# A four-layer network on one core: layer 1's preparation for batch 0 placed inside layer 0, and layer 2's first chunk prepared inside layer 1

## The chip, the cores and the metric

The kernel runs on one core of one Trainium2 chip. A core has five engines that run side by side, each with its own in-order stream of instructions: PE (TensorE, matrix products and transposes), DVE (VectorE), ACT (ScalarE), POOL (GpSimd) and SP (SyncE, which here only starts transfers). The metric is device time in microseconds of one execution; lower is better. Before the change it is 15601.95 us, the median of three runs (15600.6 to 15609.41).

## What is computed

The input is a map of 2 batches x 64 x 64 positions x 128 channels, kept as 8192 tokens of 128 numbers in float32. Four layers follow each other, and each adds its result to the map. The parts that this change touches, cut to what matters:

```python
# layer 0: group norm, projection, 3x3 depthwise convolution, then selective scans in four orders
h = dA * h + (dt * ut)[..., None] * bt          # one step of a scan, 16 states a channel, 4096 steps
y = (y - mu) * lax.rsqrt(var + eps) * ln_w + ln_b   # "layer 0's last norm"
x = x + (y * silu(z)) @ W_out.T
# layer 1: deformable 3x3 convolution on the group-normed map
offsets = conv3x3(gn(x), offset_w) + offset_b   # 9 sampling points (dy, dx) a position
val = sum over the 4 neighbours of each point: x[yi, xi] * weight
x = x + einsum('bhwkc,kcf->bhwf', val, kernel) + bias
# layer 2: layer norm of each token, then a scan over 256 channels x 256 states ...
xs = ln(t) @ W_in;  delta, B, C = xs @ W_delta, xs @ W_B, xs @ W_C
state = dA_i * state + dB_i * x_i
# ... a spectral convolution; layer 3: linear attention and a mixture of experts
```

Layer 0 treats the batches one after the other. Layer 1's sampling points of a batch need only that batch's result of layer 0.

## The kernel before the change

All text below uses the line numbers of the kernel before (L598 is line 598). The map lives in SBUF as `X`, 64 tiles of 128 tokens, 32 for each batch.

**Layer 0** (`layer0`) runs per batch `b`: a preparing stage (pools `l0p`, `l0w`: transposes, group norm, projections, the depthwise convolution, which fills `U`), the scans (pools `l0h`, `l0s`, `l0k`; an order written out by hand with `tc.manual_schedule()`), and the last norm (pools `l0f`, `l0fs`; functions `centred` and `projected`, 8 blocks of 512 tokens), which writes `X`, at L457 last. `U` is in a pool that stays for the whole layer; `Y`, the sum of the scans, has a pool of its own for each batch and lies above `U`.

**Layer 1** (`layer1`). For each batch the sampling points are made first (pool `l1p`). Transposes of `X` to channels (`to_channels`, L95, L72, L74), the bias is added to `X` (L521), group norm, transposes back to `xk` (L531), eight transfers of `xk` to a table in HBM (L539, 1 MB each in rows of 512 bytes, on SP's queue), the offset convolution (L548), and some thirty small DVE operations (L570 to L587) that end in `idx`, the table rows to fetch, and `wt`, the weights. Then comes the gather loop over the 64 tiles of tokens: nine indirect transfers from the table by POOL (L598, 128 rows of 2 KB each) into one of four buffers `G`; a DVE product with `wt` (L605); 36 PE transposes that add the four neighbours up (L612), copied out by ACT (L613); nine PE products with the kernel (L616), added to `X` by DVE (L617). At tile 36 the program also makes layer 2's mixing weights (`mixing_weights`, L693 to L711, DVE).

**Between layers 1 and 2**, `norm_tokens` takes mean and variance of all 64 tiles (L629, L630), then one set of small operations makes `rs` and `sh`; `move` (L1410) stores `X` to `x1` in HBM. Layer 2 opens its pools over the place of `X`, and `prologue` for its first chunk of 512 tokens loads `x1`, normalises, transposes, multiplies by four weights in turn (L797, L813, L822; the weights come one after the other through one buffer `w`, L806) and gives `g`, `cv`, `ea` and, through HBM, `drow`. After that `load_row` (L1127, SP) and `make_inputs` (L1139, POOL, 8.9 us) feed the first scan step (L1195, DVE).

**What sets the order.** Outside the blocks with an order written out by hand, the framework puts instructions on each engine by readiness in its own model of time, with the program's order as the priority; so independent work may be mixed. Memory is a stack of pools; a pool opened with `side="right"` takes its place from the other end. A pool that is opened on the place of a closed one waits for the use of the old one; how strictly is a question of the prediction.

Of the kernel before, what the change touches and what calls it, by code (L numbers as in the profile page):

```python
# [16 lines left out]
F32 = mybir.dt.float32  # L17
# [141 lines left out]
def layer0(k):  # L159
# [3 lines left out]
    with ExitStack() as es:  # L163
        enter = es.enter_context
        cst = enter(tc.tile_pool(name="l0c", bufs=1))
        big = enter(tc.tile_pool(name="l0b", bufs=1))
# [28 lines left out]
        U = big.tile([P, 2, L], F32, name="U")  # L195
        zs = dr.tile([2, P, B * L], F32, name="zs")

        for b in range(B):
            Xb = X[:, b * NTB : (b + 1) * NTB, :]
            with ExitStack() as e2:  # L200
# [43 lines left out]
            yb = es.enter_context(ExitStack())  # L244
            Y = yb.enter_context(tc.tile_pool(name=f"l0y{b}", bufs=1)).tile([P, 2, L], F32, name="Y")
# [175 lines left out]

            with ExitStack() as e2:
# [42 lines left out]
                projected(7, *behind)  # L465
            yb.close()
# [23 lines left out]
def layer1(k, table, mix):  # L490
# [3 lines left out]
    with ExitStack() as es:  # L494
        enter = es.enter_context
        cst = enter(tc.tile_pool(name="l1c", bufs=1))
        gp = enter(tc.tile_pool(name="l1g", bufs=4))
# [4 lines left out]
        over = enter(ExitStack())  # L502
        pre = over.enter_context(tc.tile_pool(name="l1p", bufs=1))
        w_k = cst.tile([P, 9, C], F32, name="w_k")
        nc.sync.dma_start(out=w_k, in_=ins["kern1"].rearrange("t c f -> c t f"))
        gmat = cst.tile([P, P], F32, name="gmat1")
        nc.sync.dma_start(out=gmat, in_=ins["gmat"])
        w_o = cst.tile([P, 9, 32], F32, name="w_o")
        nc.vector.memset(w_o, 0.0)
        nc.sync.dma_start(out=w_o[:, :, :18], in_=ins["offw1"].rearrange("t c f -> c t f"))  # L510
        wts, idxs = [], []
        bases = []
        for b in range(B):
            bases.append(pre.tile([P, 2, NTB, 9], F32, name="base", bufs=2))
            nc.sync.dma_start(out=bases[b], in_=ins["base"][:, :, b * NTB : (b + 1) * NTB, :])
        for b in range(B):
            Xb = X[:, b * NTB : (b + 1) * NTB, :]
            xt = pre.tile([P, L], F32, name="xt1")
            to_channels(k, ps, xt, lambda i: Xb[:, i, :], NTB)

            nc.vector.tensor_tensor(Xb, Xb, k.r("bias1").unsqueeze(1).to_broadcast([P, NTB, C]), ALU.add)  # L521
            xp = pre.tile([P, 66, 66], F32, name="xp1")
            zero_frame(nc, xp)
            groupnorm(k, pre, ps, gmat, xt, "gn1")
            nc.scalar.copy(xp[:, 1:65, 1:65], xt.rearrange("p (h w) -> p h w", w=WW))

            xk = pre.tile([P, NTB, C], F32, name="xk")
            for g in range(0, NTB, 4):
                pt = ps.tile([P, N], F32, name="pt1", tag="ps")
                for j in range(4):  # L530
                    nc.tensor.transpose(pt[:, j * P : (j + 1) * P], xt[:, (g + j) * P : (g + j + 1) * P], k.ident)  # L531
                k.copy(xk[:, g : g + 4, :].rearrange("p a c -> p (a c)"), pt)
            cells = table[b].rearrange("(y x) c -> y x c", x=TS)
            for j in range(4):
                dy, dx = divmod(j, 2)
                for yy in range(2):
                    y0 = 2 - dy + yy
                    dst = cells[y0 : y0 + 63 : 2, 2 - dx : 66 - dx, j * C : (j + 1) * C]
                    nc.sync.dma_start(out=dst.rearrange("t x c -> x t c"), in_=xk[64 * yy : 64 * yy + 64, :, :])  # L539

            off = pre.tile([P, NTB, 18], F32, name="off")
            for g in range(2):
                po = ps.tile([P, N], F32, name="po1", tag="ps")
                for t in range(9):
                    ky, kx = divmod(t, 3)
                    for j in range(4):
                        q = 4 * g + j
                        nc.tensor.matmul(po[32 * j : 32 * j + 32, :], w_o[:, t, :], xp[:, 8 * q + ky : 8 * q + ky + 8, kx : kx + WW], start=t == 0, stop=t == 8)  # L548
                ot = pre.tile([P, N], F32, name="ot1", bufs=2)
                k.copy(ot, po)  # L550
                pt = ps.tile([P, N], F32, name="pt2", tag="ps")
                for i in range(4):
                    nc.tensor.transpose(pt[:, i * P : (i + 1) * P], ot[:, i * P : (i + 1) * P], k.ident)
                nc.vector.tensor_tensor(
                    off[:, 16 * g : 16 * g + 16, :].rearrange("p (j i) o -> p j i o", i=4),
                    pt.rearrange("p (i j o) -> p j i o", j=4, o=32)[:, :, :, :18],
                    k.r("offset_b").unsqueeze(1).unsqueeze(1).to_broadcast([P, 4, 4, 18]),
                    ALU.add,
                )

            base = bases[b]
            cell = pre.tile([P, 2, NTB, 9], F32, name="cell")
            frac = pre.tile([P, 2, NTB, 9], F32, name="frac")
            rest = pre.tile([P, 2, NTB, 9], F32, name="rest")
            pt = pre.tile([P, NTB, 9], F32, name="point")
            ti = pre.tile([P, NTB, 9], I32, name="ti")
            tf = pre.tile([P, NTB, 9], F32, name="tf")
            offs = off.rearrange("p t (o a) -> p a t o", a=2)
            for a in range(2):
                nc.vector.tensor_tensor(pt, base[:, a], offs[:, a], ALU.add)  # L570

                nc.vector.tensor_copy(ti, pt)
                nc.vector.tensor_copy(tf, ti)
                nc.vector.tensor_tensor(rest[:, a], tf, pt, ALU.is_gt)
                nc.vector.tensor_tensor(tf, tf, rest[:, a], ALU.subtract)
                nc.vector.tensor_tensor(frac[:, a], pt, tf, ALU.subtract)
                nc.vector.tensor_scalar(rest[:, a], frac[:, a], -1.0, 1.0, ALU.mult, ALU.add)
                nc.vector.tensor_scalar(cell[:, a], tf, -2.0, 64.0, ALU.max, ALU.min)
            nc.vector.tensor_scalar(cell[:, 0], cell[:, 0], float(TS), float(2 * TS + 2), ALU.mult, ALU.add)
            nc.vector.tensor_tensor(tf, cell[:, 0], cell[:, 1], ALU.add)  # L580
            idx = cst.tile([P, NTB * 9], I32, name=f"idx{b}")
            nc.vector.tensor_copy(idx, tf.rearrange("p t o -> p (t o)"))
            wt = cst.tile([P, NTB * 9, 4], F32, name=f"wt{b}")
            for j in range(4):
                wy = (frac if j // 2 else rest)[:, 0]
                wx = (frac if j % 2 else rest)[:, 1]
                nc.vector.tensor_tensor(wt[:, :, j], wy.rearrange("p t o -> p (t o)"), wx.rearrange("p t o -> p (t o)"), ALU.mult)  # L587
# [977 lines left out]
```

## Time and profile before

The profiled execution took 15611.47 us; its span, from the first to the last instruction, is 15609.7 us, so 1.8 us lie around it. The median of the three timed runs is 15601.95 us. All times on the page count from the span's start.

| stretch, us | what runs | length, us |
|---|---|---|
| 0 to 2136 | layer 0, batch 0 (its last norm from 2073) | 2136 |
| 2136 to 4259 | layer 0, batch 1 (its last norm from 4196) | 2123 |
| 4259 to 4330 | layer 1 before its first gather | 71 |
| 4330 to 5316 | the 576 gathers, with all that goes beside them | 986 |
| 5316 to 5339 | the last tiles are used up | 23 |
| 5339 to 5400 | `norm_tokens`, `prologue` of layer 2's first chunk, first `make_inputs` | 61 |
| 5400 to 15300 | layer 2 | 9900 |
| 15300 to 15610 | layer 3 | 310 |

Over the span DVE is busy 88%, POOL 86%, PE 76% and ACT 63%. In a list of groups, a row gives the line, the engine, the operation, output<-inputs, the shapes, the count, then the busy time with the mean of one in ns, and the idle time ahead of them with what ended it. In a timeline a row gives start, length, engine, line, operation, names, count, and in brackets the idle time of the engine and what released it.

### The profile page before, as it was taken

The numbers are of one execution on the slowest core, as the hardware profiler recorded it, in microseconds if no ns is written. First come the engines' busy times: TensorE is split into PE (matmuls) and PEld (weight loads), VectorE is DVE, ScalarE is ACT, GpSimd is POOL, SyncE is SP. The second block draws the span as 40 slices with busy tenths as digits, with TensorE's granted clock in tenths as the row PEclk, the third lists the DMA queues.
The fourth block names the chain that finished last, engine by engine and source line by source line (L and its number), as shares of the span: only waits on it lengthen the run. The fifth ranks groups of instructions, "written<-read, shape, count | busy, mean of one in ns | idle before, by whom it ended". The sixth has DMA issues, their size and how long they took to land.

```text
span 15609.7 us, 191436 instructions
## 1 busy us (share of the span) xinstructions
PE 11894.2 (76%) x69838; PEld 7117.6 (46%) x69838; DVE 13768.3 (88%) x12194; ACT 9829.7 (63%) x15891; POOL 13474.0 (86%) x5144
## 2 busy tenths in 40 slices
PE   6666676666677645486976978979788899898897
PEld 2222232222367512154653645646445555555565
DVE  7999979999853499999999999999999999999964
ACT  5666646666410177777777777777777777777752
POOL 6888848888578699999999999999999999999960
PEclk9999999999988767697987989989999999999998
DMA  2111111211175445465655556656666666666643
GB/s 82 71 71 70 67 60 71 73 68 71 63 226 160 137 151 163 154 195 177 204 188 169 195 179 194 202 182 200 194 193 195 192 197 202 192 196 199 188 160 130
DMA packets 1211438, 2373.47 MB, mean 152 GB/s; under 512 B 346744, under 2 KB 923896, under 8 KB 1044352
## 3 DMA queue, kind: packets, MB, share of 16 engines
q1 hardware_dynamic: 1163072, 2206.74, 43.2%
q0 software_dynamic: 46560, 153.18, 3.3%
q8 instruction: 552, 9.04, 0.2%
q14 instruction: 390, 3.19, 0.1%
q10 hardware_dynamic: 864, 1.32, 0.0%
HBM read 2018.49 MB, written 342.41 MB: 151 GB/s over the span
## 4 chain that ended last, share of the span: by engine, by line
POOL 35%; PE 14%; DVE 11%; DMA 3%; ACT 2%; issue 2%; SPq 0%; POOLq 0%; ACTq 0%; DVEq 0%
POOL S L1139 34%; DVE S L1195 10%; PE pef L1023 7%; PE Z L1157 2%; PE acc L996 2%; DMA row<-drow 2%; PE pw L822 1%; POOL S L1145 1%; ACT dA L1193 1%; ACT ze L1163 1%; DMA w<-in_w_b_dram 0%; PE acc L1058 0%; DMA e<-mdr 0%; ACT e L1003 0%; DMA w<-in_w_c_dram 0%
## 5 line engine op out<-in xcount | busy, mean ns | idle before, releaser
L1195 DVE TENSOR_TENSOR_SCAN S<-dA,S 128x512 f32<-128x512 f32 x8192 | 9226.4, 1200 | 397.2 <-ACT dA L1193 208.2
L1139 POOL TENSOR_TENSOR S<-row,g 128x4096 f32<-128x4096 f32 x1024 | 9102.2, 8895 | 280.6 <-DMA row<-drow 232.4
L1193 ACT ACTIVATE dA<-row,a_t 128x512 f32<-128x512 f32 x8192 | 5616.2, 692 | 2158.3 <-DVE S L1195 2123.3
L1157 PE MATMUL Z<-S,cv 128*32 128x256 f32 x32768 | 2504.9, 436 | 1486.0 <-ACT ze L1163 1227.3
L1023 PE MATMUL pef<-hk,ur 128*128 128x256 f32 x14336 | 3507.0, 388 | 137.8 <-ACT e L1003 122.0
L1023 PEld LDWEIGHTS pef<-hk,ur 128*128 128x128 f32 x14336 | 2642.0, 191 | 1076.6 <-issue 562.1
L376 POOL TENSOR_TENSOR S<-du,br 128x1024 f32<-128x1024 f32 x1024 | 2409.7, 2356 | 282.7 <-DVE M L401 164.9
L387 DVE TENSOR_TENSOR_SCAN S<-dA,S 128x1024 f32<-128x1024 f32 x1024 | 2338.0, 2283 | 161.2 <-ACT dA L385 101.9
L1157 PEld LDWEIGHTS Z<-S,cv 128*32 128x32 f32 x32768 | 1002.0, 121 | 2695.7 <-issue 1286.1
L419 PE MATMUL yp<-M,ident 128*128 128x512 f32 x4096 | 1974.5, 604 | 2.9 <-DVE M L401 2.9
L419 PEld LDWEIGHTS yp<-M,ident 128*128 128x128 f32 x4096 | 789.9, 193 | 2147.7 <-issue 2112.7
L385 ACT ACTIVATE dA<-dt,an 128x511 f32<-128x511 f32 x2048 | 1406.5, 687 | 194.2 <-DVE S L387 148.1
L401 DVE TENSOR_TENSOR M<-S,pcn 128x1024 f32<-128x1024 f32 x1024 | 1250.4, 1221 | 151.9 <-PE pcn L343 51.9
L343 PE MATMUL pcn<-cs,sel 80*128 80x512 bf16 x1024 | 394.7, 385 | 1183.6 <-DVE M L401 1174.7
L1163 ACT COPY ze<-Z 128x512 f32<-128x512 f32 x1024 | 1123.0, 1097 | 236.9 <-PE Z L1157 204.6
L996 PE MATMUL acc<-e,mw 128*128 128x512 f32 x1920 | 1047.6, 634 | 31.2 <-ACT e L1003 30.5
L598 POOL DMA_INDIRECT G<-table,idx x576 | 810.8, 1408 | 202.6 <-issue 170.3
L1023 PEld LDWEIGHTS pef<-hd,ur 128*128 128x128 f32 x4096 | 758.2, 194 | 491.5 <-issue 236.0
L1023 PE MATMUL pef<-hd,ur 128*128 128x256 f32 (+1 forms) x4096 | 877.8, 341 | 101.6 <-ACT e L1003 95.3
L389 ACT COPY stt<-S 128x2 f32<-128x2 f32 x896 | 169.3, 189 | 1067.9 <-DVE S L387 1064.8
L605 DVE TENSOR_TENSOR G<-G,wt 128x4608 f32<-128x4608 f32 x64 | 317.6, 4963 | 579.6 <-DMA G<-table,idx 486.4
L613 ACT COPY vt<-pv 128x512 f32<-128x512 f32 (+1 forms) x192 | 88.4, 480 | 864.9 <-remote 598.0
(331 smaller groups left out, 8503.8 us busy)
## 6 DMA issues: line engine op xcount, KB each, us to landing
row<-drow SPq DMA_DIRECT2D x1024, 1024.0 KB
br<-bc SPq DMA_DIRECT2D x256, 1024.0 KB
zd<-ze SPq DMA_DIRECT2D x1024, 256.0 KB
hk<-in_phi_dram SPq DMA_DIRECT2D x128, 576.5 KB
hk<-in_phi_dram SPq DMA_DIRECT2D x96, 704.5 KB
hd<-in_phi_dram SPq DMA_DIRECT2D x512, 128.5 KB
mw<-wdr SPq DMA_DIRECT2D x480, 128.0 KB
hk<-in_phi_dram SPq DMA_DIRECT2D x160, 320.5 KB
```

The source lines that it names most:

```text
L376: nc.gpsimd.tensor_tensor(S, du, br[:, n % 4, :].unsqueeze(1).to_broadcast([P, 2, T]), ALU.mult)
L385: nc.scalar.activation(dA[:, h, rest], dt[:, h, rest], AF.Exp, scale=an[:, kk * 2 + h, n : n + 1])
L387: nc.vector.tensor_tensor_scan(flat, dflat, flat, 0.0, ALU.mult, ALU.add)
L401: nc.vector.tensor_tensor(M, S, pcn.unsqueeze(1).to_broadcast([P, 2, T]), ALU.mult)
L419: nc.tensor.matmul(yp[:, h, :], k.ident, M[:, h, :], start=False, stop=n == 15)
L996: nc.tensor.matmul(acc.rearrange("p a s -> p (a s)"), ms[f][:, o, :], e, start=box["first"], stop="whole" in box and (f, o) == todo[-1])
L1023: nc.tensor.matmul(pe[:, a, 256 - n :], ur[:, par, j, :], h[:, at : at + n], start=i == 0, stop=i + 1 == len(mm))
L1139: nc.gpsimd.tensor_tensor(S, row.unsqueeze(1).to_broadcast([P, 2, R, T]), g.unsqueeze(2).to_broadcast([P, 2, R, T]), ALU.mult)
L1157: nc.tensor.matmul(Z[32 * j : 32 * j + 32, q], cv[:, h, s], S[:, h, :, s], start=h == 0, stop=h == 1)
L1163: nc.scalar.copy(ze.rearrange("p q t e -> p q e t"), Z)
L1193: nc.scalar.activation(dA, row[:, j % R, :], AF.Exp, scale=a_t[:, h, d : d + 1])
L1195: nc.vector.tensor_tensor_scan(s, dA, s, 0.0, ALU.mult, ALU.add)
```

## The change

1. The making of the sampling points becomes a function `sampling_points`, unchanged in its operations. For batch 0, `early_points` calls it inside layer 0, right after batch 0's last norm, with a pool from the right end (`l1q`), two PSUM banks from the right end, and stores `idx` and `wt` to HBM at the end. For batch 1 it is called where both were made before.
2. The pools of the gather loop (`idx`, `wt`, `w_k`, four `G`) come from the right end and are opened inside layer 0, at the end of batch 1's last norm; batch 0's `idx` and `wt` are loaded back and the gathers of tiles 0 to 3 issued there (`early_gathers`). The loop issues tiles 4 to 63.
3. `U` gets a pool for each batch, above `Y`, closed after the scans, so that its place is free in the last norm.
4. `norm_tokens` becomes a function that is called after each tile of the loop; every fourth tile four tiles of `X` are stored to `x1`, and `rs` and `sh` are made once a batch.
5. Layer 2's first chunk is prepared at tile 40 of the loop (`first_inputs`, the same steps as `prologue`), and `g`, `cv`, `ea` go to HBM; layer 2 begins by loading them, on ACT's queue.

```diff
-def layer0(k):
+def layer0(k, beside=()):
...
-        U = big.tile([P, 2, L], F32, name="U")
...
+            yb, ub = ExitStack(), ExitStack()
+            Y = yb.enter_context(tc.tile_pool(name=f"l0y{b}", bufs=1)).tile([P, 2, L], F32, name="Y")
+            U = ub.enter_context(tc.tile_pool(name=f"l0u{b}", bufs=1)).tile([P, 2, L], F32, name="U")
...
+            ub.close()
             with ExitStack() as e2:
                 wk = e2.enter_context(tc.tile_pool(name=f"l0f{b}", bufs=3))
...
                 projected(7, *behind)
+                if beside:
+                    beside[b]()
             yb.close()
...
+class Gathers:
+    def __init__(self, k, table, es):
...
+        cst = enter(tc.tile_pool(name="l1c", bufs=1, side="right"))
...
+        self.gp = enter(tc.tile_pool(name="l1g", bufs=4, side="right"))
+    def issue(self, t):
...
+def early_points(k, table, dr, es):
+    pre = es.enter_context(tc.tile_pool(name="l1q", bufs=1, side="right"))
+    ps = es.enter_context(tc.tile_pool(name="l1qs", bufs=2, space=PSUM, side="right"))
...
+    sampling_points(k, 0, table, pre, ps, idx, wt)
...
+    nc.sync.dma_start(out=kept[0], in_=idx)
+    nc.sync.dma_start(out=kept[1], in_=wt)
...
+def early_gathers(k, table, kept, es):
+    ga = Gathers(k, table, es)
+    k.nc.sync.dma_start(out=ga.idx[0], in_=kept[0])
+    k.nc.sync.dma_start(out=ga.wt[0], in_=kept[1])
+    for t in range(4):
+        ga.issue(t)
...
-def layer1(k, table, mix):
+def layer1(k, table, ga, mix, each, first):
...
-        for b in range(B):
...
+        with tc.tile_pool(name="l1p", bufs=1) as pre:
+            sampling_points(k, 1, table, pre, ps, ga.idx[1], ga.wt[1])
         for t in range(NT):
             b, i = divmod(t, NTB)
             if t == NTB + 4 and mix is not None:
                 mix(es)
+            if t == NTB + 8 and first is not None:
+                first(es, ps)
+            if t not in ga.got:
+                ga.issue(t)
+            G = ga.got.pop(t)
...
             nc.vector.tensor_tensor(X[:, t, :], po, X[:, t, :], ALU.add)
+            if each is not None:
+                each(t)
...
+    def each(t):
+        nc.vector.bn_stats(st[:, t, :], X[:, t, :])
+        nc.vector.bn_aggr(mv[:, t, :], st[:, t, :])
+        if t % 4 == 3:
+            nc.sync.dma_start(out=out[:, t - 3 : t + 1, :], in_=X[:, t - 3 : t + 1, :])
+        if t % NTB == NTB - 1:
+            b = slice(t + 1 - NTB, t + 1)
+            rsqrt(nc, pool, rs[:, b], mv[:, b, 1], 1e-5, [P, NTB], "ln2")
+            nc.vector.scalar_tensor_tensor(sh[:, b], mv[:, b, 0], -1.0, rs[:, b], ALU.mult, ALU.mult)
...
         with tc.manual_schedule():
             got = []
-            for _ in prologue(*todo[0], got):
-                pass
-            ready[0] = got.pop()
+            xtd, g0, cv0, drow, ea0 = early
+            g, cv, ea = gc.tile([P, 2, T], F32, name="g"), gc.tile([P, 2, T], F32, name="cv"), cst.tile([P, 2, 256], F32, name="ea")
+            for dst, src in ((g, g0), (cv, cv0), (ea, ea0)):
+                nc.scalar.dma_start(out=dst, in_=src)
+            ready[0] = xtd, g, cv, drow, ea
```

## The prediction, made before the changed kernel was run

> **What bounds the kernel now.** First I read busy times by stretch (columns: stretch, length, then busy time and count of PE, PEld, DVE, ACT, POOL, clock, DMA share, GB/s), to find where layer 1 has no full engine.
>
> ```profile
> 4259.00:4330.00 71.00, 34.03 (x259) 20.15 (x260) 44.36 (x82) 11.93 (x17) 1.03 (x8) 0.74 0.56 137
> 4330.00:5316.00 986.00, 778.91 (x5784) 735.41 (x5783) 397.17 (x296) 94.51 (x197) 810.66 (x576) 0.88 0.62 184
> 5316.00:5339.00 23.00, 19.81 (x162) 19.46 (x160) 6.27 (x8) 2.88 (x6) 0.13 (x1) 0.93 0.12 34
> 5339.00:5400.00 61.00, 24.02 (x36) 8.26 (x36) 20.51 (x139) 9.83 (x17) 8.28 (x1) 0.69 0.27 97
> 4196.00:4259.00 63.00, 59.66 (x418) 50.50 (x416) 41.95 (x114) 10.83 (x17) 0.00 (x0) 0.97 0.16 50
> ```
>
> In the gather loop (986 us) POOL is busy 810.7 us, and 0.3 us of issue follow each of 576 gathers (170.3 us in the list of waits): 981 of 986, so POOL alone sets the pace. In 71 us before and 61 us after it POOL does nearly nothing: this is what can be won. The last norm (63 us) is full on PE (59.7) and empty on POOL.
>
> Why a gather tile takes 15.1 us, from the timelines of DVE and POOL:
>
> ```profile
> 4395.46 4.96 DVE L605 TENSOR_TENSOR G<-G,wt 128x4608 f32<-128x4608 f32 x1 [10.12 <-DMA G<-table,idx]
> 4395.22 0.94 POOL L598 DMA_INDIRECT G<-table,idx  x1 [0.30 <-issue]
> 4396.46 4.78 POOL L598 DMA_INDIRECT G<-table,idx  x1 [0.30 <-issue]
> 4401.55 1.00 POOL L598 DMA_INDIRECT G<-table,idx  x1 [0.31 <-issue]
> ```
>
> Eight gathers take 0.94 + 0.30 us, and the one begun under the DVE product ends only after it (4401.2 against 4400.4). The 37th gather, the first of tile 4, starts at 4387.7.
>
> What starts the loop, and layer 2:
>
> ```profile
> 4285.48 35.97 SPq L539 DMA_DIRECT2D table<-xk  x8
> 4330.09 1.07 POOL L598 DMA_INDIRECT G<-table,idx  x1 [27.37 <-DVE xt L146]
> 5386.22 1.36 SPq L1127 DMA_DIRECT2D row<-drow  x3
> 5391.72 17.59 POOL L1139 TENSOR_TENSOR S<-row,g 128x4096 f32<-128x4096 f32 x2 [75.59 <-DMA row<-drow]
> 5400.57 2.34 DVE L1195 TENSOR_TENSOR_SCAN S<-dA,S 128x512 f32<-128x512 f32 x2 [14.05 <-POOL S L1139]
> ```
>
> The points are ready at 4321, but the first gather waits for the eight table transfers, whose issue alone lasts 36 us and which land at about 4329. (The named releaser, a DVE operation done at 4329.4, gives nothing that a gather needs.) Layer 2 waits 75.6 us on POOL for a row that could be issued only when `norm_tokens` (5338.6 to 5357.3) and `prologue` (5357.8 to 5391.7) had run.
>
> How reused memory waits, at the seam of the two batches:
>
> ```profile
> 2134.98 1.13 DVE L457 SCALAR_TENSOR_TENSOR X<-po,rs,X 128x128 f32<-128x128 f32 x4 [0.90 <-PE po L453]
> 2136.24 0.34 SPq L205 DMA_DIRECT2D gmat<-in_gmat_dram  x1
> 2136.35 1.19 POOL L223 TENSOR_SCALAR dw<-ident,pv 128x128 f32<-128x128 f32 x2 [76.21 <-DVE X L457]
> ```
>
> `gmat` and `dw` need nothing of the norm, and both begin 0.2 us after its last operation. So a new pool waits for all use of every pool whose place it takes.
>
> **What the Trainium skill says.** "SBUF — State Buffer", section "SBUF size: 192, 224, or 256?": 208 KiB a partition are left on trn2; no trace shows this, and I lay out the pools with it. The same page, section "SBUF: two separate sides": DVE and GpSimd share a port pair as an exclusive lock, taken by DVE operations with two SBUF inputs or in a two-port mode. The 4.78 us gather agrees. "DMA: Bandwidth & Descriptors", section "Anatomy of one DMA", prices a transfer's fixed part at about 2.0 us; I use it for stores and reloads that the trace lacks.
>
> **Part 1, batch 0's points between the batches.** They leave 4259.5 to 4330.1, 70.6 us. Do they cost less in the new place? From the tile sizes: `l1q` holds about 77,000 bytes and lies from 136,000 to 212,992. Batch 1's preparing pool `l0p` follows what is held for longer (39,000), layer 0's constants (20,500), `Y` and `U` (32,768 each): it takes 125,000 to 182,300. They overlap, so by the seam above all of batch 1's preparation waits for the last use of `l1q`, the table transfers included. Nothing runs beside them, and batch 1's first loads stand behind the table on SP's queue. The path: norm's end to `xk` 26.0 us (4259.5 to 4285.5), table writes 43.5 (to 4329), then the two stores behind them on SP's queue, an estimate of 2 from the page's price, since the queue is already moving. Against that, seven eighths of the transposes and statistics can be done inside the norm (13.0 us before the group norm's aggregate shrink by some 4), while they add about as much PE work to a PE-bound stage (7 x 0.66 = 4.6 us). I take d = 70, from 62 to 76: the part moves, and saves nothing itself.
>
> **Part 2, gathers beside the last norm.** Thirty-six gathers need 36 x 1.25 = 45 us plus the locks; the first reload costs about 2 us. They fit in 63. What they bring along: G products of up to three tiles (5 us each) fall into DVE's gaps in the norm (63 - 42 = 21 us), lie across its chain and stretch it by 0 to 10; I take 5. Tile 4's first gather then waits for buffer 0. Its PSUM and `vt` come free only at the norm's end, then PE has 8.6 us of transposes, mixed with batch 1's own (4.4): 12 to 20, I take 14. So tile 4 starts at 4259.5 + 70 + 5 + 14 = 4348.5, against 4387.7: **39.2 us won**. The memsets of batch 1's frame, on POOL, cost 0.8 us and come before this wait.
>
> **Part 3, the loop.** Tiles 4 to 7 now meet the whole of batch 1's points. PE has 12.4 us a tile for its own work (8.6 + 3.8) and 29 for the points (transposes 4.4 and 7, convolutions 2 x 7.9, small ones 1.5); POOL asks for a buffer every 15. If the convolutions run in one piece, buffers 1 and 2 come 3 and 13 us late, if PE mixes them as at 4358, none: 0 to 16, I take 8. The points' two-input or large SBUF operations beside gathers (bias 4.4, normalising 2.4) lock POOL for 0 to 6, I take 3. The statistics of each tile, 0.43 us of DVE x 60, read one input; by the page they take no lock. The nearest row of the upper side is the mixing weights' 62 us of DVE work, beside which tiles 7 to 16 took 17 us longer than 15.1 each: 0.27 us for one, which makes 7, and 1 for the chunk's own DVE work: 0 to 8, I take 3. Stores to `x1` and the chunk's preparation lie beside the loop: 4 MB, and about 20 us of PE where PE has 2.7 spare in each tile, over 24 tiles; SP waits behind single-buffered weights, but only loads with time to spare queue there. **Loop: -14.**
>
> **Part 4, the end of layer 1.** Last `X` at 5338.7 to the first scan at 5400.6 is 61.9 us. In its place: the last store and small operations (about 4) beside the load of `g`, which needs only the place of `vt`: 3 us for 0.5 MB. A row takes 5.5 us (5386.2 to 5391.7) if it starts no earlier; `make_inputs` 8.9. I take 4.6 + 8.9 = 13.5 (11 to 17): **48.4 won**. Scales `a_t`, on the place of `X`, come within 8, before the first scan asks for them; the three loads sit on ACT's stream, where `ea` also waits for the place of `X`, but only the first scan's exponentials are queued behind it.
>
> **Sum:** 39.2 - 14 + 48.4 = 73.6 us. The profiled execution, 15611.5, becomes 15537.9; from the median 15602.0 it is **15528**. Layer 2's loop and layer 3 do the same operations.
>
> **Rivals.** (B) The pools do not keep batch 1 waiting, and the points mix with its preparation. Then about 32 us of DVE work of a batch's points add to the path in place of 70: 38 us more, 15490. For it: PE, ACT and POOL idle in 43 us of table writes. Against: the seam. (C) The order on the engines puts all of batch 1's points ahead of tile 0. Four full buffers stop POOL for 70.6 + 14 us after the norm: tile 4 at 4414.2, 26.5 later than now, with Part 3's locks of 6 -32.5 + 48.4 = +16: 15586. Against: at 4358 G's transposes come between the two convolutions. (D) Slower: gathers hold DVE out of the norm as DVE holds them. There are 14 DVE operations a block, 112 in all; with a wait w each, 112w less 21 us of idle DVE exceeds 74 from w = 0.85 us, nearly a whole gather. At 0.95: +11 us, 15613. Against, beside gathers (ns min/median/max):
>
> ```profile
> L605 DVE TENSOR_TENSOR G<-G,wt x64: 4948/4959/5030, 4350.3 to 5319.2; 128x4608 f32<-128x4608 f32 x64
> L695 DVE SCALAR_TENSOR_TENSOR smf<-m,w,smf x48: 468/477/485, 4443.9 to 4613.5; 128x256 f32<-128x256 f32 x48
> ```
>
> DVE keeps its length; POOL pays.
>
> **How the numbers follow.** Forecast 0.81, B 0.07, C 0.08, D 0.04. The forecast's bounds: all low costs, d 62, no stretch, 12, tail 11 give 54.2 + 50.9 = 105 won, 15497; all high ones, 76, 10, 20, -30, tail 17, give 22.2 - 30 + 44.9 = 37, 15565. The range, 15495 to 15566, takes these in, and leaves out B, C and D (0.19). A measurement of this kernel tells 0.2% (31 us) from no change. The forecast (even at its high end) and B are faster: 0.87 with a little of the forecast beyond its bounds taken off; C and that little within: 0.09; D 0.04.
>
> **What would show it.** Between the norm of batch 0 and batch 1's first transposes some 70 us, in which SP issues the table and DVE, ACT and PE stand still at the end; 36 gathers in the second norm; POOL waiting for buffer 0 about 14 us behind that norm; first scan of layer 2 some 13.5 us behind the last `X`. I am wrong if batch 1's preparation starts before the table is written, if POOL stands still for over 40 us after the norm, or if layer 2's scan loop changes its length (9900 us) by over 20.

## The result, and the profile after

The changed kernel takes 15571.15 us (median of 14 executions, 15561.4 to 15584.47), the kernel before 15602.28 on the same chip (14 executions): a ratio of 0.9981, 95% interval 0.9974 to 0.9988, 31 us less. The forecast was 15528 (15495 to 15566): the sign was right, the size less than half. Line numbers below are those of the kernel whose trace is shown; in the changed kernel the gathers are L589, the product with the weights L643, the transposes L650, and layer 2's first scan L1270.

Busy time by stretch in the changed kernel, with the columns of the prediction's first table:

```profile
2136.00:2211.00 75.00, 32.99 (x247) 18.49 (x245) 29.95 (x59) 8.99 (x11) 0.00 (x0) 0.71 0.51 122
4271.00:4366.00 95.00, 69.41 (x421) 57.43 (x421) 59.86 (x119) 10.72 (x17) 48.53 (x37) 0.84 0.44 142
4366.00:4411.00 45.00, 44.09 (x385) 31.31 (x386) 26.09 (x38) 11.34 (x17) 10.72 (x13) 1.00 0.41 105
5331.00:5375.00 44.00, 17.17 (x138) 16.82 (x136) 26.53 (x23) 7.00 (x11) 17.92 (x3) 0.75 0.20 59
```

The empty 71 us ahead of the gathers are now 75 us between the batches, with POOL at zero. The last norm, 65 us before, has grown to 95, and no engine is full in it any more. In the 45 us behind it TensorE is full and POOL nearly idle, although the gather loop has begun.

The waits in that norm (engine, line and what it waited for; total us, times, longest):

```profile
ACT sq L437 <- DVE yn_s L85: 55.5, 4, 16.5
POOL xp L151 <- DVE X L457: 28.0, 1, 28.0
...
PE po L453 <- DVE rs L83: 22.1, 4, 8.7
...
DVE G L643 <- DMA G<-table,idx: 21.4, 4, 8.3
```

The last row is the cause of the others: four products `G` stand in VectorE's stream inside the norm. Each waits there for its nine gathers (21.4 us together) and then takes 4.96 us, and the norm's own small steps (`yn_s`, `rs`), ready long before, stand behind. One of the four in VectorE's timeline:

```profile
4326.31 4.96 DVE L643 TENSOR_TENSOR G<-G,wt 128x4608 f32<-128x4608 f32 x1 [8.27 <-DMA G<-table,idx]
4331.18 1.12 DVE L457 SCALAR_TENSOR_TENSOR X<-po,rs,X 128x128 f32<-128x128 f32 x4
...
5357.78 16.92 DVE L896 COPY perm<-ident 128x64 f32<-128x64 f32 x2 [1.45 <-DMA x<-X]
5374.62 25.73 DVE L1270 TENSOR_TENSOR_SCAN S<-dA,S 128x512 f32<-128x512 f32 x23
```

The last two rows are the seam to layer 2. Two copies that make the small matrix `perm` take 16.9 us here, and the first scan stands behind them. In the kernel before they took 0.19 us each (ns min/median/max, then first and last start):

```profile
L767 DVE COPY perm<-ident x2: 188/192/196, 5357.9 to 5358.0; 128x64 f32<-128x64 f32 x2
```

POOL's side in the changed kernel, three places where it waits:

```profile
4378.29 0.95 POOL L589 DMA_INDIRECT G<-table,idx  x1 [11.81 <-PE pv L650]
...
4411.20 0.94 POOL L589 DMA_INDIRECT G<-table,idx  x1 [20.23 <-PE pv L650]
...
5026.69 0.94 POOL L589 DMA_INDIRECT G<-table,idx  x1 [12.64 <-PE pv L650]
```

These are the first gathers of tiles 4, 5 and 44. Each waits for a buffer that TensorE's transposes of four tiles earlier have to release. The account in the two profiled executions:

| step | kernel before | changed | won | forecast |
|---|---|---|---|---|
| first gather of tile 4 | 4387.7 | 4378.3 | 9.4 | 39.2 |
| from there to the end of the last `X` | 951.0 | 974.9 | -23.9 | -14 |
| from there to layer 2's first scan | 61.9 | 21.4 | 40.5 | 48.4 |
| sum, at the first scan | 5400.6 | 5374.6 | 26.0 | 73.6 |

From the first to the last scan of layer 2 the two profiles took 9695.3 and 9677.9 us. In the profiles of the twelve kernels below this stretch lies between 9677 and 9695 with no order in it, so the 17 us are not put down to the change; 26 us at the first scan agree with 31 between the medians.

### The profile page after: what moved, and what is told of

Same layout as the page of the kernel before. It is cut to its first block, busy times and chain, and to the rows that moved or that the text cites. A ratio compares the mean times of both kernels' runs of the same rounds, so it can differ in the third digit from the quotient of the medians.

```text
span 15565.3 us, 191484 instructions
## 1 busy us (share of the span) xinstructions
PE 11874.2 (76%) x69838; PEld 7109.2 (46%) x69838; DVE 13794.5 (89%) x12202; ACT 9836.5 (63%) x15894; POOL 13466.7 (87%) x5144
## 4 chain that ended last, share of the span: by engine, by line
POOL 36%; PE 13%; DVE 11%; DMA 3%; issue 2%; ACT 1%; SPq 0%; POOLq 0%; ACTq 0%; DVEq 0%
POOL S L1212 35%; DVE S L1270 10%; PE pef L1096 6%; PE Z L1230 2%; DMA row<-drow 2%; PE acc L1069 2%; PE pw L812 1%; POOL S L1218 1%; ACT ze L1236 0%; ACT dA L1268 0%; DMA w<-in_w_b_dram 0%; PE acc L1131 0%; ACT e L1076 0%; DMA e<-mdr 0%; PE ph L1438 0%
## 5 line engine op out<-in xcount | busy, mean ns | idle before, releaser
L1270 DVE TENSOR_TENSOR_SCAN S<-dA,S 128x512 f32<-128x512 f32 x8192 | 9225.0, 1202 | 369.2 <-ACT dA L1268 200.3
L589 POOL DMA_INDIRECT G<-table,idx x576 | 803.7, 1395 | 239.2 <-issue 166.0
L643 DVE TENSOR_TENSOR G<-G,wt 128x4608 f32<-128x4608 f32 x64 | 317.8, 4965 | 538.5 <-DMA G<-table,idx 526.2
L1076 ACT COPY e<-pef 128x512 f32<-128x512 f32 x960 | 557.9, 587 | 110.3 <-PE pef L1096 61.0
```

Of the source, the lines that this page charges most:

```text
L1270: nc.vector.tensor_tensor_scan(s, dA, s, 0.0, ALU.mult, ALU.add)
```

## The experiments

Numbers of all runs first: the ratio to the kernel before (run beside it on the same chip), and from one profile of each kernel, in us: the length of the last norm (from VectorE's last operation of the scans on); in it the time in which TensorE's matmuls of one line came 0.70 us or a multiple of it apart ("slow TensorE"); tile 4's first gather after the norm's end; tile 4 to the last `X`; and the last `X` to layer 2's first scan. The sums of slow TensorE depend on how near to a multiple a spacing has to be: between 0.02 and 0.05 us they run from 20 to 30 in e7, 27 to 33 in e4 and 5 to 8 in e5; the zeros stay.

| run | ratio (95%) | norm | slow TensorE | to tile 4 | loop | tail |
|---|---|---|---|---|---|---|
| before | 1 | 64.8 | 0 | 128.3 | 951.0 | 61.9 |
| changed | 0.9981 (0.9974 to 0.9988) | 95.1 | 0 | 12.5 | 974.9 | 21.4 |
| e1 products after norm | 0.9999 (0.9990 to 1.0007) | 99.9 | 28.7 | 16.5 | 1002.4 | 21.5 |
| e2 no early gathers | 1.0001 (0.9992 to 1.0009) | 64.4 | 0 | 65.4 | 992.5 | 22.5 |
| e3 tail alone | 0.9980 (0.9972 to 0.9988) | 64.4 | 0 | 129.7 | 971.6 | 22.3 |
| e4 wait by tile | 0.9985 (0.9979 to 0.9992) | 104.3 | 26.6 | 12.5 | 986.2 | 21.5 |
| e5 first chunk later | 0.9986 (0.9980 to 0.9993) | 95.5 | 4.9 | 12.5 | 983.7 | 21.4 |
| e6 batch 1 after tile 8 | 0.9996 (0.9987 to 1.0004) | 95.9 | 14.1 | 8.8 | 995.9 | 21.4 |
| e7 both orders | 0.9994 (0.9986 to 1.0002) | 100.7 | 23.1 | 15.2 | 992.1 | 21.5 |
| e8 paced gathers | 0.9971 (0.9960 to 0.9982) | 64.4 | 0 | 18.1 | 992.1 | 21.5 |
| e9 tail spread | 0.9977 (0.9969 to 0.9986) | 64.4 | 0 | 129.8 | 956.8 | 21.9 |
| e10 paced and spread | 0.9967 (0.9955 to 0.9979) | 64.4 | 0 | 18.1 | 980.6 | 21.5 |
| e11 pace alone | 0.9988 (0.9981 to 0.9995) | 95.1 | 0 | 14.1 | 980.8 | 21.6 |
| e12 all spread | 0.9958 (0.9944 to 0.9971) | 64.4 | 0 | 18.2 | 973.5 | 12.8 |

**Which part carries the gain: the tail alone (e3).**

```diff
-                        layer0(k, (beside0, beside1) if "1" in stages else ())
+                        layer0(k)
+                    ga.append(Gathers(k, table, e1))
@@ layer1, ahead of the loop
-            sampling_points(k, 1, table, pre, ps, ga.idx[1], ga.wt[1])
+            for b in range(B):
+                sampling_points(k, b, table, pre, ps, ga.idx[b], ga.wt[b])
```

> The kernel before with only the tail of the change: the statistics and the stores of x1 in the gather loop, layer 2's first chunk prepared there, layer 2 loading it back; both batches' points are made in layer 1, after layer 0, as before. Theory A (the whole gain of the change is its tail, 48 us less the 12 us that POOL loses at tile 44, and the early points with the early gathers bring nothing): 15566 (15556 to 15576), the changed kernel's time. Rival T (the early points and gathers bring 10 us or more that the profile of one run hides): 15580 to 15595. Rival U (the tail's gain is hidden by something in layer 2): 15595 or more.

Measured: 15579.32 against 15607.5, 0.9980, where the whole change has 0.9981. By the ratio theory A holds (its range in microseconds is missed by 3, with 15607.5 for the kernel before): the early points and gathers, the larger part of the diff, bring nothing that can be measured; the change lives on its tail.

**What the early gathers are worth where they are (e2).**

```diff
-        self.gp = enter(tc.tile_pool(name="l1g", bufs=4, side="right"))
@@ early_gathers
-    for t in range(4):
-        ga.issue(t)
@@ layer1, first line in its pools
+        ga.gp = enter(tc.tile_pool(name="l1g", bufs=4))
```

> The changed kernel with batch 0's points still made between the batches, but no gather beside the norm: the gathers' four buffers lie in memory that the norm still holds, so all 576 gathers come after it. Theory A (as made, the early gathers cost the norm as much as they win): the norm takes 65 us, the first gather comes at about 4337, tile 4 at about 4395, POOL does not starve at tile 5, and from tile 9 on the loop stands within 6 us of the changed kernel's: about 15571 (15562 to 15580). Rival (the four early tiles are worth what POOL saves, 56 us of gathers less some stall): 20 to 45 us slower, 15590 to 15615.

Measured: 15613.9, 1.0001. Theory A fails here, the rival's size is right. The norm is back at 64.4, but POOL still starves, 25.0 us ahead of tile 5 and 3.2 ahead of tile 6, so tile 9 comes at 4501 instead of 4469. That starving belongs to the early points, then, not to the early gathers: in the kernel before, batch 1's offset convolution ran from 4338 to 4369, while POOL was still filling the first four buffers, so it kept nobody waiting. Here it comes when they are full. The early points by themselves are a loss: e2's first scan of layer 2 comes 27.5 us behind e3's.

**The products taken out of the norm (e1).**

```diff
+            with tc.issue_after(k.last) if t < 4 else ExitStack():     # k.last: the norm's last VectorE instruction
                 nc.vector.tensor_tensor(V, V, ga.wt[b]..., ALU.mult)
```

> The changed kernel with one difference: VectorE's weight products of tiles 0 to 3 (the G products) are queued behind the last instruction of layer 0's last norm. Theory A (the products stand in VectorE's in-order stream inside the norm, VectorE waits there 21 us for their gathers and works 20 us on them, and the norm's own steps stand behind): the last norm takes 65 us again instead of 95, tile 4's first gather comes about 14 us after its end, near 4350 instead of 4378, and most of that stays: 35 us (20 to 45) less than the changed kernel, about 15536. Theory S (the buffers decide: the same 20 us of products, moved behind the norm, now stand together with batch 1's preparation in front of tiles 4 to 8, so POOL starves as it did): tile 5 near 4405 as now, 0 to 10 us less, 15561 to 15571.

Measured: 15612.92, 0.9999, and a norm of 99.9 us with not one product in it. Neither theory had this. VectorE no longer waits for gathers; TensorE now does something else, seen again in e7 below. Besides, POOL starves 30.5 us ahead of tile 7, since the moved products mix with batch 1's preparation.

**Batch 1's preparation put elsewhere (e6), and with the products behind the norm (e7).** In the changed kernel, what stands ahead of tile 1's transposes is seen on TensorE:

```profile
4389.37 1.04 PE L516 MATMUL pt<-ident,xt 128*128 128x128 f32 x8
4390.33 7.93 PE L533 MATMUL po<-xp,w_o 128*32 128x512 f32 x72
4398.20 1.16 PE L650 MATMUL pv<-ident,G 128*128 128x128 f32 x8
...
4400.80 7.93 PE L533 MATMUL po<-xp,w_o 128*32 128x512 f32 x72
4408.66 1.16 PE L650 MATMUL pv<-ident,G 128*128 128x128 f32 x8
```

Two blocks of batch 1's offset convolution (L533), 15.9 us, lie between parts of tile 1's transposes (L650), and tile 5's gather, at 4411.2, waits for the end of those.

```diff
-        with tc.tile_pool(name="l1p", bufs=1) as pre:
-            sampling_points(k, 1, table, pre, ps, ga.idx[1], ga.wt[1])
         for t in range(NT):
+            if t == 8:      # queued behind tile 7's last instructions on ACT, PE and DVE
+                with tc.tile_pool(name="l1p", bufs=1) as pre, tc.issue_after(vt_done), tc.issue_after(po_done), tc.issue_after(x_done):
+                    sampling_points(k, 1, table, pre, ps, ga.idx[1], ga.wt[1])
```

> The changed kernel with batch 1's preparation (its transposes, group norm, offset convolution and sampling points) queued on TensorE, ScalarE and VectorE behind tile 7's instructions instead of at the norm's end. Theory B (the 20 us for which POOL waits ahead of tile 5 are batch 1's preparation standing in the in-order queues ahead of tile 1's transposes, 16 us of offset matmuls above all, at the moment when all four buffers are full; later in the loop the queues have slack for it): the wait at tile 5 falls to 5 us or less, no wait of that size comes at tiles 10 to 14, and the time falls by 12 to 22 us, to 0.9967 to 0.9973 of the kernel before. Rival (it stalls the loop wherever it stands): POOL waits 15 to 25 us at one of tiles 10 to 14 instead, and the time stays at 0.998.

> The kernel of the run above (batch 1's preparation behind tile 7) with the products of tiles 0 to 3 queued behind the norm as well. In the run with that order alone the norm still took 100 us: TensorE issued its small matmuls at 0.7 us and multiples of it for 29 us while POOL issued its gathers without a break. Theory A' (that stall is an accident of that run and placement; the products' order is what stretches the norm): norm 65 to 75 us, tile 4 at 4350 to 4360, the time 0.9945 to 0.996 of the kernel before. Theory P (TensorE is held up whenever POOL issues early gathers without a break, and the products' order only decides whether that happens): norm 90 to 105 us again, tile 4 at 4378 or later, time 0.9965 to 0.9975, no gain over the run above.

Measured: e6 15602.09, 0.9996; e7 15600.83, 0.9994. In e6 the wait ahead of tile 5 falls from 20.2 to 3.6 us, and 14.7 us come ahead of tile 15 with 4.2 and 2.0 about it: the rival is nearest, the one piece stalls the loop here too, though at tile 15 and not at 10 to 14, and in a time above the 0.998 that the rival expected. In e7 the norm takes 100.7 us and tile 4 comes at 4386.7: theory P, though the time that it expected, 0.9965 to 0.9975, is missed. TensorE's timeline in e7's norm:

```profile
4313.77 0.16 PE L445 MATMUL pv<-mean_w,sq 128*128 128x1 f32 x1 [2.65 <-issue]
4316.57 0.16 PE L445 MATMUL pv<-mean_w,sq 128*128 128x1 f32 x1 [2.64 <-issue]
4318.71 0.16 PE L445 MATMUL pv<-mean_w,sq 128*128 128x1 f32 x1 [1.98 <-issue]
4321.50 0.16 PE L445 MATMUL pv<-mean_w,sq 128*128 128x1 f32 x1 [2.63 <-issue]
```

and POOL's gathers in that time (ns min/median/max):

```profile
L589 POOL DMA_INDIRECT G<-table,idx x36: 942/946/1302, 4278.7 to 4323.3; - x36
```

Matmuls of 0.16 us, sixteen of which take 1.84 us elsewhere in this norm, come 2.1 and 2.8 us apart, multiples of 0.70, waiting for nothing that the profile shows. Behind the first three, which take up to 1.3 us, every gather takes 0.95 us, one each 1.25 us, with no long one among them. In the changed kernel some gathers of the norm take 4.7 to 5.2 us, the ones begun under a product, and TensorE is not slow; but with products inside it was slow for 4.9 us in e5, 14.1 in e6 and 26.6 in e4, so the products' place alone does not decide it. Nor does the code of the norm, which e4, e5 and the changed kernel have in common. The changed kernel's profile has no such pause in the gather loop either, where those of all other kernels have 20 to 49 us of them behind tile 4 (spacings within 0.05 us of a multiple, after a pause of over 0.1 us for which the profile shows no cause). Whether it differs from execution to execution, one profile of each kernel cannot tell.

**The pace of the gathers (e8, e11).**

```diff
             got = self.k.nc.gpsimd.indirect_dma_start(out=G[:, o, :], ...)
+            if t < 4:
+                self.k.tc.keep_in_program_order(got)
+                self.k.tc.keep_in_program_order(self.k.nc.gpsimd.memset(self.pause, 0.0))     # 128x512, its own tile
```

> The run with both orders (products of tiles 0 to 3 behind the norm, batch 1's preparation behind tile 7), and on POOL a memset of 128x512 behind each of the 36 early gathers, which changes nothing of the result: at the 1.8 ns per element row of the 2048-wide memset's 1.8 us it takes 0.5 us, so the gathers come every 1.8 us instead of 1.25 and end near 4345. Theory P (TensorE is held up while POOL issues gathers without a break): TensorE's slow stretch shrinks from 23 us to 8 us or less, the norm takes 65 to 78 us instead of 101, tile 4 comes between 4348 and 4362 instead of 4387, the time falls to 0.9965 to 0.9978 of the kernel before. Theory D (it is the gathers' traffic, 9.4 MB in the norm, or something that has nothing to do with POOL's pace): the slow stretch stays at 15 us or more, the norm at 85 us or more, the time at 0.9985 to 1.000.

> The changed kernel with the pauses between its 36 early gathers and nothing else: the products of tiles 0 to 3 stay where they stood, in VectorE's stream inside the norm. Theory two causes (the products hold the norm up by themselves, since VectorE waits in order for gathers that now land later; TensorE's slow stretch is a second cause that took the products' place when they were moved): no slow stretch of TensorE in the norm, and still a norm of 90 to 110 us, tile 4 at 4375 or later; 0.9978 to 0.999 of the kernel before. Theory P alone (the pace was the whole cause, the products only shadowed it): norm 65 to 78 us, tile 4 before 4365, 0.997 or less.

Measured: e8 (e7 and the pauses) 15551.19, 0.9971; e11 (the change and the pauses) 15584.2, 0.9988. The stretch of the norm in e8, and then in e11:

```profile
4271.00:4336.00 65.00, 60.97 (x420) 51.18 (x420) 43.43 (x116) 10.83 (x17) 51.28 (x65) 0.97 0.61 188
```

```profile
4273.00:4368.00 95.00, 66.48 (x421) 56.01 (x421) 60.04 (x119) 10.72 (x17) 67.36 (x72) 0.86 0.46 142
```

In e8 the norm runs as if no gather were there, 61.0 of 65 us full on TensorE. The rate of the traffic is not what holds it up. The slow stretch of e7, and then a stretch of e8's norm:

```profile
4300.00:4324.00 24.00, 2.92 (x13) 3.15 (x12) 1.09 (x2) 0.00 (x0) 18.21 (x20) 0.57 0.73 209
```

```profile
4300.00:4310.00 10.00, 10.00 (x70) 8.09 (x69) 7.79 (x24) 1.15 (x2) 9.01 (x12) 1.00 0.76 238
```

TensorE works 2.9 of 24 us at a DMA share of 0.73 in the one, and all of 10 us at 0.76 in the other. The granted clock does not start it either: in e7 it was 0.86 from 4280 to 4292, with TensorE full, and 0.87 from 4292 to 4300, when the pauses began. A memset of 0.54 us after each gather, 36 instructions of pure delay on POOL, brings tile 9 from 4462 in e7 to 4429, and the medians agree: 0.9971 against 0.9994, with intervals that do not meet, is 36 us, and the two norms differ by 36.3.

e11 shows the other cause by itself, as the changed kernel's own profile does: no slow TensorE, products inside that wait 21.3 us for their gathers, and a norm of 95.1 us. (e8 and e11 differ in batch 1's place too, which by itself left the norm at 95.9 in e6.) Two causes, then, each enough for a norm of 95 to 100 us.

**The first chunk of layer 2 (e5, e9).** TensorE ahead of tile 44's gather in the changed kernel:

```profile
4989.05 2.84 PE L650 MATMUL pv<-ident,G 128*128 128x128 f32 x24
5011.98 6.73 PE L812 MATMUL pw<-xs,w 128*128 128x512 f32 x8 [20.09 <-DMA w<-in_w_b_dram]
5018.55 2.84 PE L650 MATMUL pv<-ident,G 128*128 128x128 f32 x24
```

Tile 40's transposes are cut in two by a matmul that waits 20.1 us for a weight.

```diff
 e5:
-            if t == NTB + 8 and first is not None:
+            if t == NTB + 10 and first is not None:
 e9 (on top of e3):
-    for _ in scan_inputs(k, 0, 0, x1, rs, sh, w_in, a_t, pool, pool, pool, dr, ps, got):
-        pass
+    yield from scan_inputs(k, 0, 0, x1, rs, sh, w_in, a_t, pool, pool, pool, dr, ps, got)
@@ the loop over the tiles
+            if t >= NTB + 8 and first is not None:
+                for _ in range(2):
+                    next(steps, None)
```

> The changed kernel with layer 2's first chunk prepared from tile 42 on instead of tile 40. Theory Q (the second weight matrix of the preparation is loaded on SyncE's queue behind the store of tiles 36 to 39, which waits for tile 39's result; TensorE waits 20 us for that weight with tile 40's transposes behind it, and tile 44's gathers wait 12.6 us for tile 40's buffer): with the store out of the way the wait of POOL at tile 44 or 46 falls to 5 us or less: 7 to 12 us less, 15559 to 15564. Rival C (the chain of small steps of the preparation itself holds TensorE that long): POOL's wait moves with it to tile 46 and stays 10 to 14 us: 15571.

> The run of the tail alone, with layer 2's first chunk prepared in small steps, two after each tile from tile 40 on, instead of in one piece ahead of tile 40. Theory C (POOL's 14 us at tile 44 are the piece's chain of small dependent steps in TensorE's and ScalarE's queues ahead of tile 40's transposes): no wait of POOL over 4 us from tile 40 on, the time falls by 10 to 15 us, to 0.997 to 0.9974 of the kernel before, below the changed kernel. Rival (the steps cost the same when spread, some us at each of many tiles, or the tail's end comes later): 0.9978 to 0.9985.

Measured: e5 15585.94, 0.9986. SyncE no longer holds the weight back (TensorE's longest wait there is 4.3 us), and POOL still waits, 13.6 us ahead of tile 46 instead of 12.6 ahead of tile 44: theory Q falls, the chain of small steps itself does it. A tile's transposes, which take 8.2 us where nothing comes between, are drawn out over 45.6 us in the changed kernel (tile 40) and over 34.7 in e5 (tile 42). e9: 15565.63, 0.9977; behind the first gather no wait of POOL of over 2 us, the loop 14.8 us shorter than e3's, and the first scan 17.7 us earlier than in e3, 2.5 of which it was ahead at the norm's end already. Theory C holds for the waits. The time, 0.0003 below e3's, is between the two theories, and the intervals do not tell it from e3's.

**Batch 1's wait for the early points' memory (e4).**

```diff
-                pre = e2.enter_context(tc.tile_pool(name=f"l0p{b}", bufs=1))
+                pre = e2.enter_context(tc.tile_pool(name=f"l0p{b}", bufs=1, reuse_waits="tile"))     # and l0w
```

> The changed kernel in which the tiles of layer 0's batch 1 preparation wait for the memory of the early points tile by tile instead of for the whole pool. Theory d (the whole pool is given back only when the last store of the weights has landed, 2211, and batch 1's preparation stands behind that; the tiles that it needs first were free earlier): the preparation starts between 2150 and 2195, the shift of batch 1 against the kernel before falls from 76 to 20 to 60 us, the time falls by as much, 0.9945 to 0.997 of the kernel before. Rival (the first tile lies on one that is read to the end, or TensorE and VectorE run both in program order anyway): 0 to 8 us less, 0.9975 to 0.998.

Measured: 15589.51, 0.9985; the scans of batch 1 end 3 us earlier. The rival is nearest: no gain in time can be measured, and this profile has slow TensorE in its norm besides. Small weights now start at 2188 (`dw`, 2211 before), but `xt`, the first large tile, is written at 2212.5: SyncE brings `gmat` only behind the table and the two stores (2208.9), and another place of the preparation waits until 2210.6 for the table's transfers, which read `xk` there. The seam has two keys, memory and SyncE's queue, and both open at 2210.

**Together (e10, e12).** e10 is e8 with the first chunk in small steps. e12 adds the same for batch 1's points, and moves two copies:

```diff
 e12: sampling_points yields after each group of transposes and each tap of the offset convolution
+            if t >= 8:
+                for _ in range(2):
+                    next(steps1, None)
@@ layer 2
-            nc.vector.tensor_copy(perm[:, a, :], k.ident[:, a::2][:, ::-1])
+            nc.scalar.copy(perm[:, a, :], k.ident[:, a::2][:, ::-1])
```

> The run with paced early gathers and both orders, and layer 2's first chunk prepared in small steps from tile 40 on as in the run of the tail spread. If the three losses found so far (the norm held up, TensorE's starved queue at tile 44, batch 1's preparation) are separate and add up: POOL's waits of 12.3 and 4.6 us at tiles 43 and 44 go, 14 at tile 14 stays; 12 to 17 us below the paced run, 0.996 to 0.9964 of the kernel before, the fastest of all and near the forecast of 15528. If the spread steps cost as much as they save, or what is saved early is waited for in layer 2: 0.997 to 0.9975.

> The run with paced gathers and the spread first chunk, with two more edits in different places: batch 1's preparation is made in small steps, two after each tile from tile 8 on, instead of in one piece behind tile 7; and the two small copies of layer 2's perm run on ScalarE instead of VectorE. Theory B (batch 1's offset matmuls in one piece, 16 us of TensorE, starve POOL wherever they stand): the waits of 3.5 and 14.5 us at tiles 13 and 14 go, nothing over 4 us takes their place, 12 to 20 us won by tile 18. Theory L (in the changed kernel the copies of perm take 8.2 and 8.8 us instead of 0.19, since POOL's first products of layer 2 run at the same time and VectorE cannot copy beside them; the first scan stands behind): on ScalarE they take under 1 us each and the first scan comes 13 us after the last X instead of 21.4. Both right: about 20 to 26 us less, 0.995 to 0.9956 of the kernel before. If the spread steps cost what they save: no change at tile 18; if ScalarE's copies are held as well, or something else sets the first scan: 21 us as now; both wrong: 0.9965.

Measured: e10 15552.18, 0.9967. Its loop is 11.5 us shorter than e8's, as expected, and its first scan comes 7.9 us earlier, but its median is the same as e8's. Seven and six executions that spread over 24 us do not tell a gain of this size, so the 12 to 17 us in time are not shown.

e12: 15536.99, 0.9958 (0.9944 to 0.9971), the lowest median of all, 66 us below the kernel before. The waits ahead of tiles 14 and 15 (3.5 and 14.5 in e10) are gone, with 4.0 and 4.1 ahead of tiles 17 and 21 in their place, and from tile 4 to tile 18 it needs 12.6 us less than e10. At tile 43 nothing of this is left. From tile 4's first gather to tile 43's, in e10 and then in e12:

```profile
4357.50:4990.00 632.50, 480.30 (x3789) 456.50 (x3789) 306.05 (x362) 67.76 (x137) 505.80 (x352) 0.89 0.64 194
```

```profile
4353.20:4985.80 632.60, 500.17 (x3798) 470.34 (x3797) 304.04 (x362) 67.21 (x137) 512.90 (x352) 0.87 0.65 194
```

POOL waits less, and its gathers take 512.9 us instead of 505.8. The tail falls from 21.5 to 12.8. The copies on ScalarE (ns min/median/max):

```profile
L915 ACT COPY perm<-ident x2: 243/246/249, 5331.2 to 5331.3; 128x64 f32<-128x64 f32 x2
```

Theory L holds. Theory B holds for the waits, but the small steps cost by tile 43 what they had saved by tile 18; the 7.1 us by which e12's loop is shorter all come behind tile 43, where the two kernels have the same code, and no run explains them. The two medians differ by 15 us, of which the tail is 8.7; their intervals overlap.

## Why the prediction was wrong, step by step

- **Where batch 0's points go.** "I take d = 70, from 62 to 76": batch 1's preparation starts at 2211.2, 74 us behind the norm's end at 2137.4, and its scans end 76 us later than before. Right, the pools' overlap included. e4 adds that the waiting of whole pools was not the only lock. The price of 2 us for stores and reloads was too low: the stores of `idx` and `wt` took 7.9 and 4.6 us from issue to landing, the reloads 4.7 and 5.4. The Trainium skill, "DMA: Bandwidth & Descriptors", section "Anatomy of one DMA", gives its 2.0 us for transfers that POOL issues, and these are SyncE's.
- **The step that failed.** "G products of up to three tiles (5 us each) fall into DVE's gaps in the norm (63 - 42 = 21 us), lie across its chain and stretch it by 0 to 10; I take 5." It was 30.3 us, with four products. The 21 us were no room: they are the waits of a chain in which each VectorE step is needed at once, and the engine works in order. A product placed there costs the norm its 4.96 us and the wait for its gathers too (21.4 us in all), for which I had no term: 41.2 us for the four, of which the norm's own idle time took up only 11. The changed kernel's profile and e11 show this cause alone; e8 shows the norm of 64.4 us with the products behind it. What I took for its cure, products after the norm, is worth nothing by itself (e1, e7).
- **Tile 4.** "12 to 20, I take 14" behind the norm: 12.5. Right; so of 39.2 us the stretched norm and 6 us more of d left 9.4.
- **The loop.** "If the convolutions run in one piece, buffers 1 and 2 come 3 and 13 us late": they run in two, and buffer 1 came 20.2 us late, beyond my bound of 16. TensorE was full meanwhile (it idles 0.9 us in the 32.9 from tile 4's first gather to tile 5's): both blocks, 15.9 us, and 5.6 us of batch 1's transposes went ahead of the end of tile 1's transposes, where I had buffer 1 only 3 us late. e12 removes this wait, though not its cost. "Stores to `x1` and the chunk's preparation lie beside the loop", costed at nothing beyond 1 us of VectorE: 12.6 us at tile 44. I compared 20 us of work with 2.7 us to spare in each tile; what counts is over how long the chain draws out one tile's transposes in TensorE's stream (45.6 us instead of 8.2), and there are only four buffers. e9 removes this wait. Locks and statistics, 6 us by my sum: from tile 5 to tile 43 the changed kernel gains 5.7 us on the kernel before, so they do not show.
- **The end.** "I take 4.6 + 8.9 = 13.5": 21.4. All that I named came in time; what I did not list were the two copies of `perm`, which in the kernel before lay in an idle stretch at 0.19 us. Now POOL's product starts 0.7 us ahead of them. In rival D I wrote "DVE keeps its length; POOL pays": that is the order when VectorE is first. The Trainium skill, "SBUF — State Buffer", section "SBUF: two separate sides", has both directions, since whichever starts first keeps the shared ports for its whole instruction; the trace agrees (8.2 and 8.8 us for the copies, beside POOL products of 8.8), and so does e12, 12.8 us with the copies on ScalarE.
- **The rivals.** B did not happen. C's mechanism, batch 1's points ahead of tiles whose buffers are full, happened for one tile. D's result, gathers against the norm, came nearest to what was there, though with the roles changed: VectorE waited for the landing of gathers, in its own order, and not for a lock.

## What to carry to other kernels

Idle time of an in-order engine inside a dependent chain is not room for work that itself waits: an operation put there costs its length, and its wait, to everything queued behind. Work that is to lie beside a loop with few buffers has to be cut into pieces shorter than the buffers' slack; e9 and e12 did the same work in small steps and had no long stall. Whether that wins time is seen at the end of the loop and not where the wait was: in e12 the gathers grew by as much as the waits shrank. When work is moved, list everything that lay unseen in the idle stretch that goes, down to copies of 0.2 us.

## What the runs showed of the hardware

- TensorE issued matmuls at 0.70 us and multiples of it, for some 14 to 30 us in the norms of e1, e4, e6 and e7, while POOL issued indirect gathers every 1.25 us, and waited for nothing that the profile shows. It mostly ended under a gather of 5 us (e6: the last pause ends at 4314.4, under a gather of 5.0 us from 4310.4) or behind the last gather (e7: that one ends at 4324.2, the last pause at 4329.9); in e4 a gather of 5.0 us from 4318.1 did not end it, and it lasted to 4327.2, behind the last. The kernel before has pauses of this kind too, four of 1.1 to 1.8 us in the offset convolution between 4343 and 4352.2. In the norm it was seen in five of the six kernels with early gathers and no pauses, and in none of the four with 0.54 us of memset after each gather, which move the same bytes. What TensorE and POOL's gathers share there was not found; no run isolates it.
- VectorE's copy of 128x64 took 7.1 to 8.8 us instead of 0.19 beside POOL's product of two SBUF operands, in every kernel with the changed tail that kept it on VectorE; on ScalarE, beside the same product, it took 0.25 (e12).
